# Attention and gated FFN in one kernel: order of the weight loads, of the first q and k transpositions and of the range check in the first sequence

## Chip, cores and metric

One Trainium2 chip, one core of it. The metric is the device time of one launch in microseconds (us), the median over several runs. Beside it there is one profiled execution, whose trace all durations below are taken from.

## What is computed

For each of four sequences of 512 tokens with 512 features, a layer norm feeds two branches, whose product is added to the input:

```python
xn = _layernorm(x, axis=-1)
s = _L0_attn_ref(xn, L0_attn_w_qkv, L0_attn_w_out, L0_attn_q_gamma, L0_attn_k_gamma)
g = _silu(_L0_ffn_ref(xn, L0_ffn_wq_gate, L0_ffn_s_gate, L0_ffn_wq_up, L0_ffn_s_up, L0_ffn_wq_down, L0_ffn_s_down))
x = x + s * g
```

The attention has 16 heads of 32 features: `qkv = xn @ w_qkv`; q and k are RMS-normalised per head and rotated by position; causal softmax; values; a product with `w_out`. The FFN is `down(silu(gate(xn)) * up(xn))` with 1408 hidden features; its three weight matrices come as int32 numbers with a zero point of 128 and one scale per row. All in float32.

## The kernel before

**Work and order.** One core does everything, and the order of the instructions on every engine is written out by hand (`manual_schedule`). A unit is a sequence b and a group g of four heads, 16 units in all. Each unit has two windows. In `hidden_window` PE computes a few of the 11 hidden blocks of the FFN: `hidden` (L583) with the gate weights, then with the up weights, each twice, with a coarse and a residual part of xn (`xh`, `xl`); ACT applies silu (L594), DVE multiplies (L600), ACT and POOL split the result into `h` (L601, L602). In the window that follows (`attention_window` for the first units) PE computes the scores of the unit (L450), DVE masks them and takes the row minimum (L471), ACT takes the exponential (L481), PE transposes the probabilities (L497) and multiplies them with v (L537); in between stand the FFN's down products (`contract`, L612) and the q, k, v product of the next unit (`product`, L368), whose result `rotate` normalises and rotates on ACT, DVE and POOL (L379 to L410). `Projection.turn` (L415 to L421) transposes q and k of the unit on PE, eight transpositions into two PSUM banks; ACT copies q out (L125), DVE copies k (L127). The scores need both.

**Preparing the weights.** In the first sequence the integer FFN weights are prepared beside the other work. `preparations` yields 34 blocks of up to 128x512 integers in the order in which the groups need them. `load_weights` (L241) has SP issue the load of a block into a free room (pieces of `arena`, `wout`, `oT`; the last two get their own contents later), `turn_weights` (L250) has ACT cast it to bf16 (L256) and SP issue a DMA that transposes it (L258), `finish_weights` (L261) has DVE subtract the zero point, write the result to `wgT`, `wuT` or `wdT` (L265), keep the block's largest value in a column of `largest`, and give the room back. `weights()` does a step of all three, twice in the first hidden window of the first sequence, three times in each of the next ones, and four times in each of its attention windows up to the last. A block's cast is asked for one or two steps after its load.

**Queues.** ACT, DVE, POOL and PE take their instructions in the written order; an instruction that waits holds up all behind it on its engine. SP issues almost all DMAs in the written order, too. The prologue (L933 to L966) loads x, the part of `w_qkv` for group 0, eight weight blocks, and at its end the rest of `w_qkv` for groups 1 to 3 (L961, four DMAs of 576 KB), `s_down` (L962) and three more blocks into `oT` (L963). It normalises x on DVE and POOL, transposes it on PE (`Norm.turn`, L340) and splits it (`Norm.cut`, L347: ACT writes `xh`, POOL the difference `xl`).

**First hidden window.** It has two blocks. The list `fills` (L697 to L704) says what stands between the products; in the first unit its third entry, between the gate and the up product of the second block, is `fresh.turn()` of q and k (L700). The ACT queue there reads: silu of block 0, cast of h, two casts of `oT` (L256), silu of block 1, q copy (L125), cast of h, casts of `oT` and of `wout` (L256), exponentials.

**Range check.** `find_wide` (L289) runs once, after the hidden window of group 2, when all weights are prepared: DVE takes the largest value over the columns (L293), PE transposes that one column (L295), DVE takes the largest of the 128 (L296) and writes the flag `wide` (L297). The flag decides at the end of the launch whether the whole work is done again in plain float32; with these inputs it is not. SP loads the flag into a register (L1438) right behind the load of `wout`.

Of the kernel before, what the change touches and what calls it, by code (L numbers as in the profile page):

```python
# [21 lines left out]
P = 128  # L22
# [4 lines left out]
NC = D // P  # L27
# [24 lines left out]
def interleaved(  # L52
# [27 lines left out]
    nc = tc.nc  # L80
# [23 lines left out]
    def bank_t(name):  # L104
        return ps_t.tile([P, 512], F32, tag="t", name=name)
# [50 lines left out]
    def load_wqkv(groups):  # L156
        for c in range(NC):
            nc.sync.dma_start(
                wqkv[:, c, :, groups, :],
                w_qkv[ts(c, P), :].rearrange("p (i g d) -> p i g d", i=3, g=NC)[:, :, groups, :],  # L160
            )
# [23 lines left out]
    def load_scales():  # L185
        srow = work("srow")
        at = 0
        for s in (s_gate, s_up):
            n = s.shape[0] // P
            nc.sync.dma_start(srow[at : at + n, 0:P], s.rearrange("(c p) -> c p", p=P))  # L190
            at += n
        return srow, at

    sdown = const.tile([P, D], F32, name="sdown")
# [46 lines left out]
    def load_weights(n):  # L241
        for _ in range(n):
            if todo and rooms:
                src, k, dst, name = todo.pop(0)
                room = rooms.pop(0)
                raw = room[:, : k * P]
                nc.sync.dma_start(raw.bitcast(U32), src.bitcast(U32))
                loaded.append((now[0], room, raw, k, dst, name))
# [29 lines left out]
    def weights(n=2):  # L278

        now[0] += 1  # L280
        for _ in range(n):
            if turning and now[0] - turning[0][0] >= 2:
                finish_weights()
        load_weights(n)
        for _ in range(n):
            if loaded and now[0] - loaded[0][0] >= 1:
                turn_weights()

    def find_wide():  # L289

        assert len(finished) == n_prep
        row = small.tile([P, 1], F32, tag="row", name="largest_row")
        nc.vector.tensor_reduce(row, largest, AX.X, ALU.max)  # L293
        tp = bank_t("largest_t")
        nc.tensor.transpose(tp[0:1, 0:P], row, ident)  # L295
        nc.vector.tensor_reduce(row[0:1, :], tp[0:1, 0:P], AX.X, ALU.max)  # L296
        nc.vector.tensor_single_scalar(wide, row[0:1, :], EXACT_MAX, ALU.is_ge)  # L297

    units = [(b, g) for b in range(B) for g in range(NC)]

# [122 lines left out]
    def swapped(b, g):  # L423


        return units[NC - 1] <= (b, g) < units[-1]
# [149 lines left out]
    def hidden(b, f, i, other=False):  # L576

        assert "gu"[i] + f"_{f}" in finished
        bank = (bank_t if other else bank_a)(f"h{i}_{b}_{f}")
        w = (wgT, wuT)[i]  # L580
        for a in (xh, xl):
            for c in range(NC):
                nc.tensor.matmul(  # L583
                    bank,
                    lhsT=w[:, c, ts(f, P)],
                    rhs=a[:, c, :],
                    start=(c == 0 and a is xh),
                    stop=(c == NC - 1 and a is xl),
                )
        return bank  # L590

    def gate(b, f, bank):
        sil = work(f"sil_{b}_{f}")
        nc.scalar.activation(sil, bank, AF.Silu, scale=scales[:, f : f + 1])  # L594
        return sil

    def gated(sil, f, bank, to):

        up = scales[:, NF + f : NF + f + 1]
        nc.vector.scalar_tensor_tensor(sil, bank, up, sil, ALU.mult, ALU.mult)  # L600
        nc.scalar.copy(to[:, 0, :], sil)  # L601
        nc.gpsimd.tensor_tensor(to[:, 1, :], sil, to[:, 0, :].bitcast(F32), ALU.subtract)  # L602
# [76 lines left out]
    def hidden_window(b, g, last, fresh, result, norm, beside):  # L679

        placed = last is not None and last.placed
        if result is not None and not placed:
            result.gate(0)

        def drain(i):
            if last is not None and not placed:
                last.turn(i, scalar=False)
                last.turn(i + 1, scalar=True)  # L690

        def turned(*tiles):
            if norm is not None:
                for t in tiles:
                    norm.turn(t)

        fills = [  # L697
            lambda: drain(0),
            lambda: drain(2),
            lambda: (last.spread_sums() if last is not None else None, fresh.turn()),  # L700
            lambda: turned(0, 1),
            lambda: turned(2),
            lambda: turned(3),
        ]  # L704
        for i, f in enumerate(chunks[g]):
            bank = hidden(b, f, 0, other=placed and i == 0)
            sil = gate(b, f, bank)
            if placed and i == 0:
                last.blocks(0, 1, 2)
            if fills:  # L710
                fills.pop(0)()
            if result is not None:
                for t in ((), (0, 1))[i] if placed else (2 * i + 1,):
                    result.gate(t)
            bank = hidden(b, f, 1, other=placed and norm is None and f == chunks[g][-1])
            gated(sil, f, bank, h[:, i])
            if placed and i == 0:
                last.blocks(3)
                last.spread()
            if fills:  # L720
                fills.pop(0)()
            if result is not None:
                for t in ((), (2, 3))[i] if placed else ((2,), ())[i]:
                    result.gate(t)
            for e in beside[i]:
                e()
            if b == 0:
                weights()
        if last is not None:
            last.turn_sums()  # L730
            if not placed:
                last.values()
# [200 lines left out]
    def prologue():  # L933
        norm, fresh = Norm(0), Projection(0, 0)
        load_weights(4)
        scales_in = load_scales()
        load_weights(4)
        for t in range(NT):
            norm.stats(t)
            norm.roots(slice(t, t + 1))  # L940
            if t:
                norm.apply(t - 1)
                norm.turn(t - 1)
        norm.apply(NT - 1)
        norm.turn(NT - 1)
        prepare_table()
        for t in range(NT):
            norm.cut(t)
        for _ in range(4):
            turn_weights()  # L950
        fresh.product(0)
        fresh.rotate(0)
        for _ in range(4):
            turn_weights()
        for t in range(1, NT):
            fresh.product(t)
            fresh.rotate(t)
            if t > 1:
                finish_weights()
                finish_weights()  # L960
        load_wqkv(slice(1, NC))  # L961
        nc.sync.dma_start(sdown, s_down.partition_broadcast(P))  # L962
        load_weights(3)  # L963
        now[0] += 1
        prepare_scales(*scales_in)
        return fresh  # L966

    fresh, last, norm, done = prologue(), None, None, None
    for u, (b, g) in enumerate(units):
        result = Result(b - 1) if g == 0 and b else None  # L970
        done = result or done
        beside = [[], [], []]
        if g == NC - 2 and b + 1 < B:
            for t in range(NT):
                load_x(b + 1, t)
            norm = Norm(b + 1)
            beside[1] += [lambda t=t: norm.stats(t) for t in (0, 1)]
            beside[2] += [lambda t=t: norm.stats(t) for t in (2, 3)]
            beside[2].append(lambda: norm.roots(slice(0, NT)))
        if g == NC - 1 and b + 1 < B:  # L980
            for i, tiles in enumerate(((0, 1), (2, 3))):
                beside[i] += [lambda t=t: norm.apply(t) for t in tiles]
        due = norm if g == NC - 1 and b + 1 < B else None
        hidden_window(b, g, last, fresh, result, due, beside)
        if g == 1 and b:
            for t in range(NT):
                done.store(t)
        if (b, g) == (0, NC - 1):
            nc.sync.dma_start(wout, w_out.rearrange("(c p) m -> p c m", p=P))
        if (b, g) == (0, NC - 2):  # L990
            find_wide()
        s = steps(b, g, fresh.v)
        if u + 1 == len(units):
            break
        fresh = Projection(*units[u + 1])
        if swapped(b, g):
            placed_window(b, g, last, s, fresh, due, result)
        else:
            attention_window(b, g, last, s, fresh, due)
        last = s[3]  # L1000
# [476 lines left out]
```

## Time and profile before

| | us |
|---|---|
| median of 3 runs | 678.67 (678.5 to 678.67) |
| the profiled execution, its own time | 679.54 |
| its span | 677.7 |

| first 180 us of the profiled execution | us |
|---|---|
| SP issues the loads of w_qkv for groups 1 to 3 (L158) | 27.75 to 30.39 |
| last q and k product of group 0 ends on PE | 26.25 |
| first hidden product starts | 26.34 |
| first scores of group 0 start | 42.09 |
| first hidden product of group 1 starts | 69.29 |
| first scores of group 1 start | 84.74 |
| first scores of group 2 start | 127.34 |
| first scores of group 3 start | 168.32 |

A profile line of a group reads: line, engine, operation, what it writes and reads, how many; in a timeline the start and the duration stand in front, and brackets at the end give the idle time of that engine just before and who ended it. A line of the waits reads: who waited for whom, us in total, how often, the longest. `PEclk` is the granted clock of TensorE, as a share of full speed. The page has further sections: a picture of 40 slices of 16.9 us, the DMA queues, and the chain of work that ended last.

### The profile page before, as it was taken

Reading aid. Unit: us, or ns where it says so; the run is one execution under the profiler, and the core shown is the slowest. Engines: PE = TensorE matmul, PEld = TensorE weight load, DVE = VectorE, ACT = ScalarE, POOL = GpSimd, SP = SyncE. Lnnn points to the kernel's source line nnn. Section 1 sums busy time; section 2 is a strip of 40 time slices with the busy share of each in tenths; the row PEclk is TensorE's granted clock in tenths of the full one; section 3 lists DMA queues with packets and bytes.
Section 4 is the critical chain, followed back from the end, with each engine's and each line's share of the span. In section 5 each row is a group of like instructions: output and inputs, shape, how many; then the busy total and the mean of one; then the engine's idle time right before and its main releaser. Section 6 shows DMA issues by size and latency. Waiting matters only on the chain.

```text
span 677.7 us, 11804 instructions
## 1 busy us (share of the span) xinstructions
PE 640.3 (94%) x4050; PEld 430.7 (64%) x4050; DVE 443.5 (65%) x1208; ACT 364.6 (54%) x931; POOL 319.9 (47%) x369
## 2 busy tenths in 40 slices
PE   4969999999999999999999999999999999999995
PEld 2645766668665576767665576766766466676752
DVE  3547677764886366777688357777588565757663
ACT  3456576554765064565757046464757246464660
POOL 4913536254472723537283641727284442726522
PEclk9969999999999999999999999999999999999998
DMA  7583644200222144322013323312223304222401
GB/s 250 149 209 94 180 97 107 94 1 1 48 55 68 50 124 100 74 47 46 22 43 79 94 44 106 102 46 48 64 47 78 94 1 125 47 63 48 125 1 68
DMA packets 48560, 53.19 MB, mean 78 GB/s; under 512 B 21334, under 2 KB 31852, under 8 KB 48492
## 3 DMA queue, kind: packets, MB, share of 16 engines
q1 hardware_dynamic: 47532, 51.93, 30.3%
q8 instruction: 34, 0.56, 0.3%
q10 hardware_dynamic: 960, 0.43, 0.2%
q14 instruction: 34, 0.28, 0.1%
HBM read 21.80 MB, written 4.19 MB: 38 GB/s over the span
## 4 chain that ended last, share of the span: by engine, by line
PE 84%; ACT 4%; DVE 4%; DMA 2%; POOL 2%; issue 2%; SPq 1%; DVEq 0%; ACTq 0%
PE qkv L368 25%; PE h L583 23%; PE dn L612 11%; PE so L655 8%; PE pv L537 6%; PE sc L450 5%; PE pt L497 4%; PE qkt L420 2%; POOL h L602 1%; DMA oT<-in_L_ffn_wq_up 1%; ACT arena L125 1%; DVE sil L600 1%; ACT arena L481 1%; PE xnt L344 1%; DMA x<-in_L_attn_x 1%
## 5 line engine op out<-in xcount | busy, mean ns | idle before, releaser
L481 ACT ACTIVATE arena<-arena,least 128x128 f32<-128x128 f32 (+3 forms) x256 | 141.2, 553 | 66.4 <-DVE least L471 66.3
L368 PE MATMUL qkv<-wqkv,xnT 128*128 128x384 f32 x512 | 173.6, 492 | 2.3 <-DVE least L471 2.3
L368 PEld LDWEIGHTS qkv<-wqkv,xnT 128*128 128x128 f32 x512 | 96.6, 193 | 68.6 <-issue 5.8
L471 DVE CUSTOM_DVE_ANT_0 arena<-sc,mask 128x128 f32<-128x128 f32 (+3 forms) x256 | 109.5, 486 | 31.0 <-PE sc L450 30.8
L408 POOL TENSOR_TENSOR qk<-qk,qs 128x256 f32<-128x256 f32 x64 | 46.7, 730 | 149.3 <-DVE qs L403 149.3
L602 POOL TENSOR_TENSOR h<-sil,h 128x512 fp32r<-128x512 f32 x44 | 57.8, 1314 | 116.2 <-ACT h L601 114.8
L315 POOL TENSOR_TENSOR ss<-ss,minus_half 128x8 f32<-128x8 f32 x64 | 106.7, 1668 | 5.3
L612 PE MATMUL dn<-wdT,h 128*128 128x512 f32 x352 | 100.0, 422 | 1.8 <-POOL h L602 1.8
L514 DVE STREAM_TRANSPOSE arena<-arena 128x384 f32<-128x384 f32 (+1 forms) x96 | 88.6, 977 | 12.3 <-PE pt L497 7.5
L612 PEld LDWEIGHTS dn<-wdT,h 128*128 128x128 f32 x352 | 63.5, 191 | 40.2 <-issue 20.4
L379 ACT ACTIVATE squares<-qkv 128x256 f32<-128x256 f32 x64 | 24.5, 382 | 119.7 <-PE qkv L368 99.0
L400 DVE TENSOR_TENSOR qk<-qkv,tab 128x256 f32<-128x256 f32 x64 | 27.0, 423 | 74.8 <-ACT v L380 74.4
L600 DVE SCALAR_TENSOR_TENSOR sil<-h,scales,sil 128x512 f32<-128x512 f32 x44 | 32.6, 740 | 56.8 <-PE h L583 45.0
L601 ACT CAST h<-sil 128x512 fp32r<-128x512 f32 x44 | 27.3, 620 | 69.8 <-DVE sil L600 69.8
L655 PE MATMUL so<-wout,oT 128*128 128x512 f32 x128 | 58.2, 593 | 0.0
L450 PE MATMUL sc<-kT,qT 32*128 32x512 f32 (+3 forms) x512 | 49.8, 474 | 5.8 <-ACT qT L125 5.8
L583 PE MATMUL h<-xh,wuT 128*128 128x512 f32 x176 | 50.1, 406 | 1.5 <-ACT qT L125 1.5
L497 PE MATMUL pt<-ident,arena 128*128 128x128 f32 x304 | 43.6, 279 | 7.2 <-ACT arena L125 7.1
L583 PE MATMUL h<-xh,wgT 128*128 128x512 f32 x176 | 49.1, 401 | 0.0
L497 PEld LDWEIGHTS pt<-ident,arena 128*128 128x128 f32 x304 | 35.0, 142 | 21.2 <-ACT arena L125 10.5
L583 PE MATMUL h<-xl,wuT 128*128 128x512 f32 x176 | 48.1, 395 | 0.0
L583 PE MATMUL h<-xl,wgT 128*128 128x512 f32 x176 | 48.1, 395 | 0.0
(90 smaller groups left out, 907.2 us busy)
## 6 DMA issues: line engine op xcount, KB each, us to landing
arena<-arena SPq DMA_DIRECT2D x48, 256.0 KB, 4.7
arena<-arena SPq DMA_DIRECT2D x48, 192.0 KB, 3.6
x<-in_L_attn_x SPq DMA_DIRECT2D x16, 256.0 KB, 4.7
out<-o SPq DMA_DIRECT2D x15, 256.0 KB, 4.5
xr<-in_L_attn_x SPq DMA_DIRECT2D x12, 256.0 KB, 4.1
wqkv<-in_L_attn_w_qkv SPq DMA_DIRECT2D x4, 576.0 KB, 4.8
wout<-in_L_ffn_wq_up SPq DMA_DIRECT2D x6, 256.0 KB, 3.1
wout<-in_L_ffn_wq_down SPq DMA_DIRECT2D x5, 256.0 KB, 3.9
```

What stands on the lines that cost most here:

```text
L315: nc.gpsimd.tensor_tensor(dst, dst, minus_half[:, : dst.shape[-1]], ALU.pow)
L368: nc.tensor.matmul(bank.rearrange("p (i d) -> p i d", i=3), lhsT=xnT[:, c, ts(t, P)], rhs=wqkv[:, c, :, self.g, :], start=(c == 0), stop=( ...
L408: nc.gpsimd.tensor_tensor(qk, qk, qs, ALU.add)
L450: nc.tensor.matmul(bank, lhsT=qT[rows, ts(self.t, P)], rhs=kT[rows, : self.keys], start=True, stop=True,)
L471: nc.vector.tensor_tensor_reduce(out=pr, in0=self.banks[j], in1=mask[:, N - self.keys :], scale=float(HD), scalar=3.0e38, op0=ALU.add, op1 ...
L481: nc.scalar.activation(pr, pr, AF.Exp, bias=least, scale=-1.0, accum_out=self.sums[:, self.t, j : j + 1],)
L497: nc.tensor.transpose(tp[:, ts(i * (self.t + 1) + k, P)], self.probs[n * self.per + i][:, ts(k, P)], ident,)
L514: nc.vector.transpose(piece(self.way, self.t + 1)[:, : HPG * self.keys].rearrange("p (c m k) -> p c m k", c=4, k=32)[:, :, j * n : (j + 1) * n
L583: nc.tensor.matmul(bank, lhsT=w[:, c, ts(f, P)], rhs=a[:, c, :], start=(c == 0 and a is xh), stop=(c == NC - 1 and a is xl),)
L602: nc.gpsimd.tensor_tensor(to[:, 1, :], sil, to[:, 0, :].bitcast(F32), ALU.subtract)
L612: nc.tensor.matmul(bank, lhsT=h[:, i, a, ts(t, P)], rhs=wdT[:, f, :], start=(i == 0 and a == 0), stop=(f == fs[-1] and a == 1),)
L655: nc.tensor.matmul(self.banks[t], lhsT=oT[:, g, ts(t, P)], rhs=wout[:, g, :], start=(g == 0), stop=(g == NC - 1),)
```

## The change

It touches four things, all in the first sequence. (1) The loads of w_qkv are parted by group: group 1 stands behind the three weight blocks at the end of the prologue instead of in front of them; group 2 and `s_down` follow after the first hidden window, group 3 after the second. (2) In the first unit q and k are turned at the end of the hidden window, after both blocks, instead of inside the second. On PE the eight transpositions thereby stand behind the eight products of the up half of block 1; on ACT the q copy stands behind the cast of h and the casts of `oT` and `wout`; on DVE the k copy stands behind the second L600 and two L265. (3) `find_wide` becomes a generator with two stops: its first reduction stays after the hidden window of group 2, the transposition and the rest come after the hidden window of group 3. (4) The prologue's `xl` is computed on DVE instead of POOL. Nothing is added to or taken from the arithmetic; SP issues 8 more DMAs (12 of 192 KB in place of 4 of 576 KB).

```diff
@@ find_wide
         nc.vector.tensor_reduce(row, largest, AX.X, ALU.max)
+        yield
         tp = bank_t("largest_t")
         nc.tensor.transpose(tp[0:1, 0:P], row, ident)
         nc.vector.tensor_reduce(row[0:1, :], tp[0:1, 0:P], AX.X, ALU.max)
         nc.vector.tensor_single_scalar(wide, row[0:1, :], EXACT_MAX, ALU.is_ge)
+        yield
@@ hidden_window
-            lambda: (last.spread_sums() if last is not None else None, fresh.turn()),
+            lambda: (last.spread_sums(), fresh.turn()) if last is not None else None,
...
-        if last is not None:
+        if last is None:
+            fresh.turn()
+        else:
             last.turn_sums()
@@ prologue
         for t in range(NT):
-            norm.cut(t)
+            norm.cut(t, nc.vector)
...
-        load_wqkv(slice(1, NC))
-        nc.sync.dma_start(sdown, s_down.partition_broadcast(P))
         load_weights(3)
+        load_wqkv(slice(1, 2))
@@ the loop over the units, after hidden_window
         if (b, g) == (0, NC - 1):
+            next(finding)
             nc.sync.dma_start(wout, w_out.rearrange("(c p) m -> p c m", p=P))
+        if b == 0 and 2 + g < NC:
+            load_wqkv(slice(2 + g, 3 + g))
+        if (b, g) == (0, 0):
+            nc.sync.dma_start(sdown, s_down.partition_broadcast(P))
         if (b, g) == (0, NC - 2):
-            find_wide()
+            finding = find_wide()
+            next(finding)
```

## The prediction

> **What bounds the kernel now.** I read the page first (busy shares, the 40 slices, the chain), then the waits of PE, then the timelines of the stretches where PE stood still, then a table of windows for the granted clock.
>
> ```profile
> PE 640.3 (94%) x4050; PEld 430.7 (64%) x4050; DVE 443.5 (65%) x1208; ACT 364.6 (54%) x931; POOL 319.9 (47%) x369
> PEclk9969999999999999999999999999999999999998
> ```
>
> PE carries the kernel; what it does not fill is 37 us. Slice 3 of PEclk (33.9 to 50.8 us) is the one dip before the end. The waits of PE between 20 and 180 us name what an edit in the first sequence can reach:
>
> ```profile
> PE sc L450 <- ACT qT L125: 5.8, 1, 5.8
> PE qkv L368 <- DVE least L471: 2.3, 4, 0.8
> PE largest_t L295 <- DVE largest_row L293: 1.2, 1, 1.2
> PE qkt L420 <- POOL qk L410: 1.1, 1, 1.1
> ```
>
> The timeline around the first (start, duration, engine, line) shows why ACT was late:
>
> ```profile
> 27.75 2.64 SPq L158 DMA_DIRECT2D wqkv<-in_L_attn_w_qkv  x4
> 30.43 0.66 SPq L962 DMA_DIRECT2D sdown<-in_L_ffn_s_down  x1
> 31.14 0.46 SPq L247 DMA_DIRECT2D oT<-in_L_ffn_wq_gate  x1
> 35.14 1.10 PE L583 MATMUL h<-xl,wuT 128*128 128x512 f32 x4
> 39.70 1.27 ACT L256 CAST oT<-oT 128x512 bf16<-128x512 uint32 x2 [6.86 <-DMA oT<-in_L_ffn_wq_gate]
> 41.46 0.57 ACT L125 COPY qT<-qkt 128x512 f32<-128x512 f32 x1
> 42.09 1.96 PE L450 MATMUL sc<-kT,qT 32*128 32x128 f32 x16 [5.85 <-ACT qT L125]
> ```
>
> ACT's next job is the cast of a weight block that queues behind 2.36 MB of wqkv and 0.26 MB of sdown; the q copy stands behind that cast on ACT, and PE's scores behind the q copy. PE idles from 36.24 to 42.09 us. That stall also costs clock:
>
> ```profile
> core 0: us, PE busy (x) PEld busy (x) DVE busy (x) ACT busy (x) POOL busy (x), PEclk, DMA share, GB/s
> 31.42:34.83 3.41, 2.33 (x15) 1.83 (x14) 2.38 (x6) 0.62 (x1) 3.29 (x3) 1.00 1.00 343
> 34.84:38.25 3.41, 1.40 (x6) 0.77 (x5) 0.26 (x1) 0.00 (x0) 0.00 (x0) 1.00 1.02 307
> 38.25:41.66 3.41, 0.00 (x0) 0.00 (x0) 0.07 (x1) 1.92 (x4) 0.00 (x0) 0.50 0.84 309
> 41.66:45.07 3.41, 2.98 (x19) 2.14 (x20) 3.17 (x15) 3.05 (x5) 1.27 (x1) 0.50 0.98 122
> 45.08:48.49 3.41, 3.41 (x12) 2.72 (x11) 1.72 (x7) 3.40 (x16) 0.00 (x0) 0.50 0.96 197
> 48.49:51.90 3.41, 3.41 (x13) 2.05 (x12) 1.32 (x3) 1.08 (x5) 0.00 (x0) 1.00 0.00 0
> ```
>
> The clock halves at 38.25 us, 2.0 us into the gap, and comes back at 48.49: three times 3.41 us apart, so it changes on a grid of 3.41 us. A stretch 68% busy kept the full clock, one 41% busy lost it; one 87% busy did not win it back, one wholly busy did. From 42.09 to 48.49 PE works at half speed: the 16 sc take 1.96 us (0.94 in the next group's window), eight dn 3.71 (8 x 0.234 = 1.87 at full clock).
>
> **The change, part by part.** Sums are against the profiled execution: 679.54 us, span 677.7. The runs' median, 678.67, lies 0.87 below it; the saving is carried over unchanged.
>
> *Queue.* The three oT loads are issued at 27.75 instead of 31.14. Data began to move at about 29.5 and ran at 321 to 336 GB/s in the next 4 us, so the 0.79 MB are in by about 32. ACT finishes its h cast (L601) at 32.22 + 0.62 = 32.84: its wait of 6.86 us goes. After them SP issues the first wqkv group (4 x 0.62 us, until about 31.7), then the wout block that frees at 32.81. 0.79 + 0.26 MB after 32 give a landing near 35.2.
>
> *Turning q and k later.* PE: the eight h matmuls of the second up block move ahead of the eight qkt. They start at 32.04 and take 2 x 0.93 us, to 33.9; POOL's last qk ends at 33.55, so the 1.07 us that PE waited there go too; qkt takes 0.87, to 34.8. ACT: after 32.84 two casts (1.27) to 34.11, sil 0.68 to 34.8, DVE's sil (L600) 0.75 to 35.6, h cast to 36.1, oT cast to 36.6, wout cast to 37.2 (pitch 0.52, as at 42.38 to 43.42), q copy 0.57 to 37.75. The change puts the q copy behind the casts of oT and of that wout block: the added wait is ACT's on the wout load (35.2, needed at 36.6; 1.4 us of cover; if the cover goes, q copy, scores and all of PE are late by the excess). DVE: wdT twice after 35.6, then the k copy, to about 37.5. Scores start at 37.8 instead of 42.09, and PE's gap is 34.8 to 37.8: 3.0 us.
>
> *The clock in that gap.* Here a rule and the row differ. The Trainium skill (TensorE: Matmul & The Clock Gate, Part 1, What's actually happening) has the clock drop after a wholly idle window of about 3.4 us, and says that the grid's place varies from run to run. By the rule a gap of 3.0 us costs no clock. The rows above show a drop after a stretch that was 41% busy. The runs lie within 0.17 us, though a grid in another place would move the half-speed time by up to 1.7 us; so I keep the grid. The gap then fills 34.84 to 38.25 but for 0.5 us: 15% busy, the clock falls at 38.25. The next stretch, to 41.66, is wholly busy if the scores start at 37.8, and the clock comes back there. By the rows: half of sc at full speed, the rest to 39.2; 5.2 dn at half speed to 41.66, 2.8 at full to 42.3; pt 0.45 (its exponentials are done by 40.7: table load 37.75 to 39.0, four of 0.39); qkv 2.6 to 45.35. Before, that product ended at 51.19: 5.85 us saved. By the rule it ends at 43.7 (pt waits for ACT until 41.1): 7.5 saved.
>
> *Does it last?* After 51.19 ACT had waited 2.33 us and DVE 1.93 for this product, so neither becomes the bound sooner. From there to 69.3 PE, DVE and ACT hand on to each other at full clock; no 3.41 us of that stretch are under 78% busy, so a shift against the grid costs no clock. All transfers hang on instructions that shift along.
>
> *The search parted.* At group 2 PE idles 1.24 us, as the transposition stands ahead of the scores and DVE does two st/mv pairs first:
>
> ```profile
> 124.81 1.08 PE L537 MATMUL pv<-arena,v 128*32 128x128 f32 x32
> 127.14 0.27 PE L295 MATMUL largest_t<-ident,largest_row 128*1 128x128 f32 x1 [1.24 <-DVE largest_row L293]
> 127.34 0.94 PE L450 MATMUL sc<-kT,qT 32*128 32x128 f32 x16
> ```
>
> Now the scores follow pv at 125.9. dn's last h part (POOL, done 127.31) is due at 126.7 + 5 x 0.234 = 127.9; ACT's table is in at 127.74, exponentials end by 129.3, pt needs them at 129.7. So 1.45 us are saved. The transposition (0.2) comes back at group 3, where its row is long done and DVE idles 1.91 us before the first mask. Net 1.25 us; between 0.9 and 1.45. From 127 to 175 the chain is nearly all PE, so it lasts. SP's load of the flag (L1438) now waits until about 169; behind it stand the arena copies, due only at 179.65.
>
> *At nothing.* xl on DVE: four of 0.68 (DVE's L351 later on) instead of 4.97 us of POOL, in DVE's idle 5.58 us before 19.20; POOL's qk sum started at 20.10 on DVE's sine products anyway. Were that cover gone, 2.7 us. The wqkv groups 2 and 3: 2.5 us of SP and 2.4 of DMA each at 330 GB/s, sdown 0.66. SP has nothing to issue from 47.2 to 53.6 and from 89.0 to 94.7, and the products that read them come 40 us later. Without cover the next weight loads would be 3 us late. 512-byte pieces instead of 1536: the first group, in such pieces, moved among other loads at 288 to 370 GB/s (4 to 8 us), so no price; half that rate would land the wout block near 38.3 and cost 1.7.
>
> **Sum.** 5.85 + 1.25 = 7.1: 672.4 for a profiled execution, 671.6 for the median.
>
> **Rivals.** (1) Clock back one stretch later, at 45.08, if sc does not count as fully busy or starts after 38.3: dn to 42.95, pt to 43.8, two qkv matmuls at half speed, six at 0.324: 47.0, 4.2 saved, + 1.25: 673.2. For it: the 87% stretch with sc in it did not win the clock back. Against: it began with 0.43 us of idle. (2) Clock never falls (grid elsewhere, or the gap shorter): 7.5 + 1.25: 670.0. Against it the 41% row. (3) Part of the wait returns, on ACT's weight casts or later in the group: 3 us kept, 675.7. (4) The change does nothing: the q copy waits as long for wout as it did for oT: within 0.2% of 678.7. (5) Slower: the same place, ACT's cast of the wout block ahead of the q copy. Scores start 1.2 us after that load lands. If it lands after 42.1, they start at 43.3 and the gain, search included, is gone; each us beyond is lost whole, and at 44.5 the time is 681. That needs 1.05 MB in 10 us, 100 GB/s where the trace shows over 320.
>
> **How the numbers follow.** Chances: forecast 0.47 (670.9 to 672.4 alone), (1) 0.23, (2) 0.13, (3) 0.08, (4) 0.03, (5) 0.06. A time within 0.2% (1.4 us) is what a measurement here can't tell from no change. The range takes in (2) and (1) with their bounds: 669.8 to 674.8. Faster 0.91, same 0.03, slower 0.06.
>
> **What would show it.** In the profile after: ACT's oT cast at about 32.8 without a wait; no wait of PE for POOL at qkt; sc near 37.8; PEclk at one half from 38.25 to 41.66 and nowhere else before the end; no wait of PE at largest_t; sc of group 2 straight behind pv. It is wrong if ACT's wout cast waits for its load, if the half clock lasts to 45, or if DVE or ACT, not PE, sets the pace from 40 to 46 us.

## The result and the profile after

| | before | after |
|---|---|---|
| median of 6 runs each, us | 678.67 (677.74 to 678.96) | 672.66 (669.79 to 673.74) |
| profiled execution, its own time / span, us | 679.54 / 677.7 | 673.09 / 671.3 |
| first hidden product of group 0 starts | 26.34 | 24.96 |
| first scores of group 0 | 42.09 | 37.16 |
| first hidden product of group 1 | 69.29 | 63.85 |
| first scores of group 2 | 127.34 | 120.45 |
| first scores of group 3 | 168.32 | 161.86 |

The ratio is 0.9908 (95% interval 0.989 to 0.9926): 6.0 us less. The single runs after lie 4 us apart, those of before 1.2; the shortest (669.79) has a mean granted clock of 0.997, the three longest (673.09 to 673.74) have 0.992. A stretch of 3.41 us at half speed takes 0.5 x 3.41 / 671 = 0.0025 off a run's mean clock, so by this estimate the ends differ by two such stretches.

From here on the changed file's lines stand two further down (L450 is now L452, L612 is L614). The page of the kernel after, busy shares and granted clock:

```profile
PE 639.0 (95%) x4050; PEld 429.9 (64%) x4050; DVE 446.2 (66%) x1212; ACT 364.6 (54%) x931; POOL 315.1 (47%) x365
PEclk9979999999999999999999999999999999999998
```

Slice 3 still dips, to 7 instead of 6: the clock still falls. The waits of PE between 20 and 180 us, after:

```profile
PE sc L452 <- ACT qT L125: 3.3, 1, 3.3
PE qkv L370 <- DVE least L473: 2.3, 4, 0.8
PE pt L499 <- ACT arena L125: 0.2, 1, 0.2
PE largest_t L296 <- ACT xnT L347: 0.2, 1, 0.2
```

The wait for POOL at `qkt` is gone, the one for DVE at `largest_t` has become 0.2 us for another engine. The scores still wait for the q copy, 3.3 us instead of 5.8. The timelines of SP, ACT and PE around it, after:

```profile
28.80 2.57 SPq L158 DMA_DIRECT2D wqkv<-in_L_attn_w_qkv  x4
31.46 0.55 SPq L247 DMA_DIRECT2D wout<-in_L_ffn_wq_up  x1
31.37 1.13 ACT L256 CAST oT<-oT 128x512 bf16<-128x512 uint32 x2
36.00 0.62 ACT L256 CAST wout<-wout 128x512 bf16<-128x512 uint32 x1 [0.96 <-DMA wout<-in_L_ffn_wq_up]
36.52 0.58 ACT L125 COPY qT<-qkt 128x512 f32<-128x512 f32 x1
37.16 1.66 PE L452 MATMUL sc<-kT,qT 32*128 32x128 f32 x16 [3.30 <-ACT qT L125]
38.75 3.78 PE L614 MATMUL dn<-wdT,h 128*128 128x512 f32 x8
```

The cast of `oT` has no bracket: its 6.86 us are gone. The cast of `wout`, which the q copy now stands behind, waits 0.96 us for a load that SP issued at 31.46, behind the four w_qkv loads of group 1: 4.5 us to landing. Eight dn take 3.78 us, as before: half speed. A table of windows of 3.41 us, cut 0.15 us ahead of the places where the clock changed (start and end, length, busy time of PE, PEld, DVE, ACT and POOL with their instructions, granted clock, DMA share, GB/s):

```profile
32.42:35.83 3.41, 1.35 (x10) 0.78 (x8) 2.56 (x6) 1.80 (x4) 3.08 (x3) 1.00 1.23 290
35.83:39.24 3.41, 2.08 (x17) 1.43 (x18) 0.40 (x3) 2.45 (x4) 0.04 (x1) 0.52 1.19 200
39.24:42.65 3.41, 3.41 (x10) 2.53 (x10) 2.59 (x15) 2.79 (x13) 0.00 (x0) 0.50 1.38 159
```

By the trace's record of the clock it falls at 35.98, in the gap, and comes back at 42.81, so it was low for two stretches, the second of them wholly busy. PE works at half speed from 37.16 to 42.81, 5.65 us (before: 42.09 to 48.49, 6.4). The edges do not lie where those of before lay.

The parted search, in PE's timeline of groups 2 and 3, after:

```profile
119.44 1.08 PE L539 MATMUL pv<-arena,v 128*32 128x128 f32 x32
120.45 0.94 PE L452 MATMUL sc<-kT,qT 32*128 32x128 f32 x16
...
161.66 0.27 PE L296 MATMUL largest_t<-ident,largest_row 128*1 128x128 f32 x1 [0.16 <-ACT xnT L347]
161.86 0.94 PE L452 MATMUL sc<-kT,qT 32*128 32x128 f32 x16
```

Group 2's scores follow pv directly; the transposition stands in group 3.

**Where the 6.4 us of the profiled execution went.** The first hidden product starts 1.38 us earlier; from there to the first hidden product of group 1 it takes 38.89 us instead of 42.95 (4.06); scores of group 1 to those of group 2 41.10 instead of 42.60 (1.50 saved), group 2 to 3 41.41 instead of 40.98 (0.43 given back). 1.38 + 4.06 + 1.50 - 0.43 = 6.51; 0.05 went back between the first hidden product and the first scores of group 1, and the remaining 0.06 later. The 1.38 is mostly no effect of the change. The first q, k, v product starts 0.50 us earlier (13.25 instead of 13.76) and takes 0.88 less (11.60 instead of 12.48); the clock came to full speed at 15.50 in this execution and at 17.78 in the one before. In kernels without the move of `xl` the first hidden product started between 24.61 and 26.34, in those with it between 24.81 and 25.87.

### The profile page after: what moved, and what is told of

It reads as the page before. It is cut to its first block, busy times and chain, and to the rows that moved or that the text cites. A ratio compares the mean times of both kernels' runs of the same rounds, so it can differ in the third digit from the quotient of the medians.

```text
span 671.3 us, 11815 instructions
## 1 busy us (share of the span) xinstructions
PE 639.0 (95%) x4050; PEld 429.9 (64%) x4050; DVE 446.2 (66%) x1212; ACT 364.6 (54%) x931; POOL 315.1 (47%) x365
## 4 chain that ended last, share of the span: by engine, by line
PE 85%; ACT 5%; DVE 5%; issue 2%; DMA 2%; POOL 2%; SPq 0%; DVEq 0%; ACTq 0%
PE qkv L370 25%; PE h L585 24%; PE dn L614 11%; PE so L657 8%; PE pv L539 6%; PE sc L452 5%; PE pt L499 4%; PE qkt L422 2%; POOL h L604 1%; ACT arena L125 1%; DVE sil L602 1%; ACT arena L483 1%; PE xnt L346 1%; DMA x<-in_L_attn_x 1%; DMA wout<-in_L_ffn_wq_up 1%
## 5 line engine op out<-in xcount | busy, mean ns | idle before, releaser
L614 PE MATMUL dn<-wdT,h 128*128 128x512 f32 x352 | 100.0, 422 | 1.8 <-POOL h L604 1.8
L614 PEld LDWEIGHTS dn<-wdT,h 128*128 128x128 f32 x352 | 63.5, 191 | 40.2 <-issue 21.0
L452 PE MATMUL sc<-kT,qT 32*128 32x512 f32 (+3 forms) x512 | 49.5, 474 | 3.3 <-ACT qT L125 3.3
```

The lines of the kernel that those rows point to most:

```text
L452: nc.tensor.matmul(bank, lhsT=qT[rows, ts(self.t, P)], rhs=kT[rows, : self.keys], start=True, stop=True,)
L614: nc.tensor.matmul(bank, lhsT=h[:, i, a, ts(t, P)], rhs=wdT[:, f, :], start=(i == 0 and a == 0), stop=(f == fs[-1] and a == 1),)
```

## The experiments

The theory going in: the load order gives the gain, the search about 1 us, and the later turning by itself costs, since the q copy then stands behind the casts of two blocks, one of them late. What the gap costs beyond its length is the clock behind it. The rival: the later turning helps, and part of the gain is its own.

Useful for reading all runs: from the first hidden product of group 0 to that of group 1 (H), the first scores, and whether the clock fell.

| kernel | median us (runs) | ratio, 95% | first hidden / first scores | H | clock low |
|---|---|---|---|---|---|
| before (its first profile) | | | 26.34 / 42.09 | 42.95 | 38.3 to 48.5 |
| e1 load order alone | 672.15 (5) | 0.9917, 0.9904 to 0.9931 | 25.99 / 35.73 | 36.39 | never |
| e2 search alone | 676.88 (20) | 0.9986, 0.9978 to 0.9994 | 24.66 / 41.26 | 42.91 | 39.0 to 45.8 |
| e3 later turning alone | 680.4 (5) | 1.004, 1.0027 to 1.0054 | 24.64 / 43.84 | 45.36 | 38.1 to 48.4 |
| e4 after, turned ahead of the casts | 669.97 (4) | 0.9886, 0.9871 to 0.9901 | 24.81 / 34.92 | 35.96 | never |
| f1 after again | 672.77 (5) | 0.9923, 0.991 to 0.9937 | 25.36 / 37.44 | 39.18 | 37.1 to 43.9 |
| f2 after, gap filled | 670.18 (4) | 0.9883, 0.9868 to 0.9898 | 25.14 / 37.01 | 35.97 | never |
| f3 after, old place of turning | 671.44 (4) | 0.9903, 0.9888 to 0.9918 | 25.87 / 35.59 | 36.80 | never |
| f4 after, wout load ahead of w_qkv | 671.23 (4) | 0.9896, 0.9881 to 0.9911 | 24.96 / 36.10 | 36.81 | 36.3 to 39.7 |
| g1 both mends | 668.88 (4) | 0.9861, 0.9846 to 0.9876 | 25.06 / 35.16 | 35.12 | never |
| g2 before, gap filled | 678.97 (13) | 1.0008, 0.9999 to 1.0016 | 24.61 / 42.83 | 44.68 | 45.2 to 48.7 |
| g3 before, oT loads ahead, rest whole | 678.44 (13) | 1.0003, 0.9995 to 1.0012 | 25.60 / 35.54 | 41.83 | 44.2 to 47.7 |
| g4 xl on DVE alone | 678.14 (13) | 0.9991, 0.9983 to 1.0 | 25.37 / 41.87 | 43.19 | 40.4 to 47.2 |

The runs of one letter were made on one chip beside runs of the kernel before (medians 677.77, 677.87 and 678.47). "Clock low" is read from the one trace of each kernel, ahead of the fall at the very end. The mean clocks of the single runs agree: all runs of e1, e4, f2, f3 and g1 have 0.997 or more, those of the kernel before 0.989 to 0.994.

**e1 and e2, one part alone.** e1 takes the new load order into the kernel before:

```diff
-        load_wqkv(slice(1, NC))
-        nc.sync.dma_start(sdown, s_down.partition_broadcast(P))
         load_weights(3)
+        load_wqkv(slice(1, 2))
...
+        if b == 0 and 2 + g < NC:
+            load_wqkv(slice(2 + g, 3 + g))
+        if (b, g) == (0, 0):
+            nc.sync.dma_start(sdown, s_down.partition_broadcast(P))
```

> Only the order of the loads is changed; q and k are turned inside the second block as before. Theory (the saving is the load order's, and the later turning costs part of it): ACT's wait for the oT load goes, the q copy is done before PE ends the up products, PE's gap ahead of the first scores shrinks from 5.85 us to under 1 us, the clock stays full, and the first product of the next group ends about 6.7 us earlier: 672.0 us, all but the search of the whole gain or more. Rival (the later turning is needed too): PE still waits for POOL at qkt and for a bank or the q copy at the scores, 3 to 4 us saved, about 675.

e2 takes the two stops of `find_wide`:

```diff
+        yield
         tp = bank_t("largest_t")
...
+            next(finding)
```

> Only the search for large weights is parted. Theory: the 1.45 us between pv and the scores of group 2 go, and about 0.45 us come back at group 3: 1.0 us saved, 677.7 us. Rival (another engine sets the pace there): the scores start earlier but PE waits later in the window for DVE or ACT, nothing saved: 678.7 us.

Measured: 672.15 and 676.88. The load order alone gives 5.6 us, nearly all that the whole change gave; the search 0.9. Together that would be 6.5, and the whole change gives 6.0 in the first measurement and 5.1 in f1. The waits of PE in e1 between 20 and 60 us:

```profile
PE qkv L368 <- DVE least L471: 1.4, 2, 0.8
PE qkt L420 <- POOL qk L410: 1.0, 1, 1.0
PE sc L450 <- DVE sil L600: 0.5, 1, 0.5
PE dn L612 <- DVE wdT L265: 0.3, 1, 0.3
```

Of the 5.8 us in front of the scores 0.5 are left, with work on either side; the wait for POOL is the old one (1.1 before). The clock stays full.

**e3, the later turning alone.**

```diff
-            lambda: (last.spread_sums() if last is not None else None, fresh.turn()),
+            lambda: (last.spread_sums(), fresh.turn()) if last is not None else None,
...
-        if last is not None:
+        if last is None:
+            fresh.turn()
+        else:
             last.turn_sums()
```

> Only the turning of q and k is moved behind both hidden blocks; the loads stay in the old order. Theory: the q copy now stands behind two more casts, one of them of a wout block that is the last in the queue; the scores start 2.5 us or more later than before (about 44.6 instead of 42.1 us): about 681 us. Rival (turning later saves the 1.07 us that PE waits for POOL and the q copy was never what PE waited for): 677.6 us.

Measured: 680.4, slower than before. PE's wait for the q copy is now

```profile
PE sc L450 <- ACT qT L125: 10.3, 1, 10.3
```

In the old load order ACT's silu of block 1 stands behind the cast of the late `oT` block (here at 38.96). Now the cast of h and two more casts stand ahead of the q copy as well: it starts at 43.22 instead of 41.46, and the scores at 43.84 instead of 42.09. PE's wait grows by more than that, since its up products are done before it.

**e4, the turning between its old and its new place:** behind both blocks' products, ahead of the last casts.

```diff
                 e()
+            if last is None and i == len(chunks[g]) - 1:
+                fresh.turn()
             if b == 0:
                 weights()
-        if last is None:
-            fresh.turn()
-        else:
+        if last is not None:
             last.turn_sums()
```

> The changed kernel with one difference: q and k are turned behind the second block's products but ahead of the casts of the last two weight blocks, so ACT's q copy does not stand behind the cast that waits for the wout load. Theory: the scores start about 2 us earlier than in the changed kernel (35.1 instead of 37.2 us), the gap of PE is 1.7 us and half a grid stretch stays busy, so the clock stays full; PE then waits some 1.5 us for the exponentials; about 3.4 us less than the changed kernel: 669.2 us. Rival (the clock falls all the same, or the wait for wout only moves to the exponentials and costs as much): 672 us.

Measured: 669.97, 2.8 us below f1 (on another chip; against the kernel before on the same chip e4 saves 7.8 us and f1 5.1). Here PE waits 1.36 us in front of the scores, and for a different engine:

```profile
34.92 0.94 PE L452 MATMUL sc<-kT,qT 32*128 32x128 f32 x16 [1.36 <-DVE wdT L265]
```

The 16 sc take 0.94 us: full clock. So the late place on PE is good (H 35.96 against 36.80 in f3, at the old place); the place behind ACT's casts is bad.

**f1, the changed kernel again, and f2, its gap filled** with 12 products of 128x512 behind the turning:

```diff
         if last is None:
             fresh.turn()
+            idle = ps_d.tile([P, D], F32, tag="dn", name="idle")
+            for k in range(12):
+                nc.tensor.matmul(idle, lhsT=wgT[:, 0, 0:P], rhs=xh[:, 0, :], start=True, stop=True)
```

> The changed kernel unaltered, to see its spread. Theory (the time left over from the turn's gap is set by where the clock's grid falls on it): about 672.6 us, single runs 669.8 to 673.8, and a run is shorter the higher its mean granted clock. Rival (the spread comes from the loads, not from the clock): the same median, but runs of one mean clock as far apart as all of them.

> The changed kernel, with twelve 128x512 products (2.8 us at full clock) put on PE behind the turning of q and k, into a bank that nobody reads: their result is not used, and they fill most of the 3.3 us gap. Theory (the gap costs clock behind it: scores to the q, k, v product at half speed for up to 5.5 us, worth up to 2.7 us): clock full until the end, about 670.2 us, all runs within 1 us. Rival (the clock is a symptom, ACT or DVE sets the pace from the scores on): 672.6 or above.

Measured: 672.77 with single runs of 672.17 to 673.73, and 670.18 with runs of 669.81 to 670.45. The scores start equally late in both, 12.08 and 11.87 us behind the first hidden product: in f2 PE still has no useful work in the gap. Yet from those scores to the scores of the next token tile f1 takes 10.22 us and f2 7.21. The windows of f1:

```profile
33.60:37.01 3.41, 0.36 (x4) 0.12 (x2) 2.48 (x6) 1.87 (x4) 1.62 (x2) 1.00 1.13 235
37.01:40.42 3.41, 2.98 (x19) 2.10 (x20) 1.28 (x10) 2.62 (x7) 0.00 (x0) 0.51 1.80 210
40.42:43.83 3.41, 3.41 (x11) 2.73 (x10) 1.85 (x8) 2.75 (x12) 0.00 (x0) 0.50 0.73 177
```

and of f2:

```profile
33.60:37.01 3.41, 2.95 (x15) 2.06 (x13) 2.27 (x6) 2.28 (x5) 1.71 (x2) 1.00 1.42 235
37.01:40.42 3.41, 3.41 (x29) 2.68 (x30) 2.46 (x14) 3.37 (x12) 0.00 (x0) 1.00 1.07 203
```

The same 3.41 us, 11% busy in one and 87% in the other. That the clock, not DVE or ACT, sets the pace behind the gap is thereby shown: 3.0 us of the profiled execution, 2.6 of the median. f1's own spread (1.6 us) did not settle the expectation that a shorter run always has a higher mean clock: four of its runs, 672.59 to 673.73, all have 0.992; the fifth and shortest, 672.17, has 0.995.

**f3, the whole change but the old place of turning** (the reverse of e3's diff):

> The changed kernel with q and k turned at the old place, inside the second block; load order, parted search and xl on DVE as changed. Theory (the later turn by itself costs, since the q copy now stands behind two casts that wait for data): queue 672.15 less the search's 0.9, 671.2 us, runs within 1 us, clock full. Rival (the later turn takes away the wait of PE for POOL and so helps): above 672.7.

Measured: 671.44, runs of 671.19 to 671.72, all below f1's shortest (672.17). So in this company the later turning costs 1.3 us at the median. But it does so through the clock: with the clock full (f2) H is 35.97, less than f3's 36.80.

**f4, the wout load ahead of the w_qkv loads of group 1:**

```diff
         load_weights(3)
-        load_wqkv(slice(1, 2))
...
         load_weights(n)
+        if behind is not None:
+            behind()
...
-                weights()
+                weights(behind=(lambda: load_wqkv(slice(1, 2))) if g == 0 and i == 0 else None)
```

> The changed kernel with the w_qkv loads of group 1 issued behind the first wout block's load instead of in front of it; all else as changed. Theory (ACT's wait of 0.96 us for the wout block, which the q copy stands behind, comes from those four loads in front): no wait at that cast, scores about 1 us earlier, gap 2.3 us, 671.3 us (670 to 672.3, by the clock). Rival (the wout block is late by its own transfer): wait stays near 1 us, 672.6 us.

Measured: 671.23. ACT's wait is gone, the q copy starts at 35.47 and the gap is 2.52 us. The clock falls in it all the same, but the scores (36.10) start before the next stretch begins, and it is back at 39.70:

```profile
32.88:36.29 3.41, 0.89 (x11) 0.65 (x13) 2.56 (x6) 2.57 (x6) 2.38 (x2) 1.00 0.91 295
36.29:39.70 3.41, 3.41 (x21) 2.37 (x20) 1.31 (x11) 2.80 (x10) 0.00 (x0) 0.50 1.12 124
```

One stretch at half speed here, two in f1 and in the first profile after. Scores to scores of the next tile: 8.78 us, between f2's 7.21 and f1's 10.22.

**g1, both mends together** (the diffs of e4 and f4):

> The changed kernel with both mends: q and k turned behind the products of both blocks but ahead of the last casts of weights (as in the run e4), and the w_qkv loads of group 1 behind the first wout block's load (as in f4). Theory: ACT's wait of 0.74 us at the wout cast in e4 goes, so the exponentials and the first transposed probabilities come 0.7 us earlier: 669.3 us, runs within 0.6 us, clock full. Rival (that wait lay beside DVE's masks or PE's products): 669.97 as e4.

Measured: 668.88, runs of 668.38 to 669.63; ratio 0.9861 (0.9846 to 0.9876), the best version, ahead of both kernels. The casts no longer wait; what is left is PE's 1.50 us for DVE's `wdT` in front of the scores:

```profile
35.16 0.94 PE L454 MATMUL sc<-kT,qT 32*128 32x128 f32 x16 [1.50 <-DVE wdT L265]
```

**g2, the kernel before with its gap filled** by 22 such products behind the hidden products of the first unit (the same lines as in f2).

> The kernel before, with 22 products of 128x512 (5.15 us at full clock) put on PE behind the hidden products of the first unit, into a bank that nobody reads: their result is not used, and they fill most of the 5.85 us gap. It keeps the wait and takes away the clock's fall. Theory (from the first scores to those of the next token tile before took 10.3 us, and 7.2 with the clock full in f2): 3.1 us less than before, 674.8 us. Rival (behind the gap DVE and ACT set the pace): within 0.5 us of before.

Measured: 678.97, no gain: the theory's 3.1 us did not come, and the rival's number did. In the profiled execution the first hidden product came 1.73 us earlier than in the profile before and the load of `oT` no earlier, so the gap was 7.6 us and the filling covered 5.3. The clock fell at 45.24, behind the first scores. Windows cut at its own edges:

```profile
38.42:41.83 3.41, 2.15 (x10) 1.39 (x8) 0.00 (x0) 1.32 (x3) 0.00 (x0) 1.00 0.61 223
41.83:45.24 3.41, 2.03 (x20) 1.39 (x20) 2.91 (x14) 3.05 (x6) 1.28 (x1) 1.00 0.48 100
45.24:48.66 3.42, 3.42 (x11) 2.75 (x11) 2.13 (x10) 3.41 (x14) 0.00 (x0) 0.50 0.83 208
```

From the first scores to the end of the next q, k, v product it took 8.37 us instead of 9.10, but the scores came 0.74 us later (42.83), behind a later `oT`. Nor could f2's 3.1 us carry over. In the old order ACT has the cast of h, two casts of blocks and a table load to do between the q copy and the first exponential, which starts 3.26 us behind the first scores in the kernel before and in g2, and 1.28 in f2 (in this order):

```profile
45.35 0.40 ACT L481 ACTIVATE arena<-arena,least 128x128 f32<-128x128 f32 x1
46.09 0.40 ACT L481 ACTIVATE arena<-arena,least 128x128 f32<-128x128 f32 x1
38.29 0.40 ACT L483 ACTIVATE arena<-arena,least 128x128 f32<-128x128 f32 x1
```

PE's transpositions need four of them. An estimate from the rows of before: the fourth ends at 46.91, the last transposition (0.2) and the product (2.6) follow, 49.7 instead of 51.19; a full clock would have been worth some 1.5 us there. Three of g2's thirteen runs have a mean clock of 0.998 or 0.999, as high as where it never fell, and took 677.81, 678.14 and 679.06: none near 674.8. Why they gained nothing at all is not shown, as only one execution has a trace.

The second of g2's windows, 60% busy, lost the full clock; in g1 one that was 56% busy kept it:

```profile
33.03:36.45 3.42, 1.92 (x24) 1.30 (x23) 2.89 (x9) 2.59 (x6) 2.26 (x2) 1.00 0.92 291
```

So the busy share of PE alone does not say when it falls.

**g3, the three oT loads ahead, w_qkv and s_down whole behind them:**

```diff
-        load_wqkv(slice(1, NC))
-        nc.sync.dma_start(sdown, s_down.partition_broadcast(P))
         load_weights(3)
+        load_wqkv(slice(1, NC))
+        nc.sync.dma_start(sdown, s_down.partition_broadcast(P))
```

> The kernel before with only the three oT loads moved in front of the w_qkv loads of groups 1 to 3 and s_down, which stay whole (2.36 MB and 0.26 MB) and stay there. Theory (the loads in front of the first wout block decide: 2.03 MB more than in e1, some 6 us at 340 GB/s): the q copy is early, but the exponentials stand behind ACT's cast of the wout block, which lands near 43 us; PE's transposition of the probabilities waits about 5 us and the clock falls: 676 to 678 us. Rival (the three oT loads are all that matters): 672.2 as e1.

Measured: 678.44, the same as before. ACT's next cast takes the wait over, and the exponentials stand behind it:

```profile
41.63 0.62 ACT L256 CAST wout<-wout 128x512 bf16<-128x512 uint32 x1 [3.98 <-DMA wout<-in_L_ffn_wq_up]
```

So moving three loads to the front gives nothing; the gain needs what stands behind them parted and put off, w_qkv of groups 2 and 3 and s_down: 1.57 + 0.26 = 1.83 MB (the expectation's 2.03 was miscounted).

**g4, `xl` on DVE alone** (`norm.cut(t)` becomes `norm.cut(t, nc.vector)` in the prologue):

> The kernel before with only xl moved from POOL to DVE in the prologue. Theory (DVE has room there and the next step waits for other work): same as before, 677.9 us within 0.5. Rival (q and k are ready earlier or DVE is late): over 1 us off, to either side.

Measured: 678.14, 0.3 us below the kernel before; the interval of the ratio reaches from a gain of 1.2 us to none. So the move is worth little or nothing, as forecast.

## Why the prediction was right, and where it was not

The direction, the place and the range were right: 672.66 in 669.8 to 674.8, 1.1 us above 671.6. Of the forecast's 7.1 us its own steps gave 5.1 in the profiled execution (4.06 + 1.07), and f1 measures 5.1 as well; the 6.0 of the first medians has an interval of 5.0 to 7.5. By its steps:

- **Queue.** Right: no wait at the `oT` cast. e1 shows it alone, 5.6 us.
- **No wait for POOL at `qkt`.** Right, but what it frees on PE is lost in front of the scores.
- **"1.4 us of cover" for the wout load.** Wrong: a wait of 0.96 us. In the profiled execution ACT came for the block at 35.04 and not 36.6 (the prologue was quicker by 1.4), and the block landed at 36.0 and not 35.2. 1.4 - 1.56 - 0.8 = -0.96. It was foreseen as a thing to watch ("it is wrong if ACT's wout cast waits for its load"). Half the DMA rate, feared for the 512-byte pieces, did not come: 290 GB/s in that stretch, 307 in the nearest one before.
- **Scores at 37.8.** 11.46 us behind the first hidden product in the forecast, 12.20 measured; PE's gap is 3.3 us instead of 3.0.
- **"So I keep the grid."** This is the step that failed. The edges lie elsewhere in every profile: the clock fell at 38.26 before, 35.98 after, 37.11 in f1, 36.30 in f4, which leaves 0.7, 1.8, 3.0 and 2.2 modulo 3.41. The Trainium skill (TensorE: Matmul & The Clock Gate, Part 1, What's actually happening) says that the window is free-running and its place varies between runs; on that it was right and the forecast, which rejected it, was not. The forecast's reason was that the runs of before lie within 0.17 us. Those were three runs. All six of the first comparison lie within 1.2 us, the 33 beside g within 2.6, and their mean clock is not one either: six have 0.989 (678.67 to 679.80), the others 0.992 to 0.994 (677.23 to 678.97). So the time at half speed varied in the kernel before, too. The execution that the forecast summed against (679.54, 0.989) was of the slower kind, and carrying its whole saving over to the median left that out.
- **What makes the clock fall.** The forecast took the row (41% busy, lost) over the same section's wholly idle window, and this held: after, a stretch 35% busy between the clock's own edges lost it (40% as cut in the table), in f4 one of 26%. Counted over all fourteen traces with windows laid on each trace's edges, the 2638 that kept the full clock were all at least 50% busy, and of the 23 that lost it 22 were at most 41% busy; the other is g2's, 60%. On the way back 90% busy was not enough (f1), and wholly busy was, in all nine cases.
- **"Back at 41.66", 3.41 us at half speed.** Its size failed: 6.8 us low, of which 5.65 with work, because the scores came after the edge at 35.98 and so the first stretch was partly idle. That is what rival (1) described, and the product ended 20.79 us behind the first hidden product, not 19.01: 4.06 us saved instead of 5.85, near its 4.2. 0.74 of the 1.79 between them is the later scores; the other 1.05, by subtraction, is the clock. f4 shows the forecast's own case. (The eight dn of before took 3.78 us by the trace, not 3.71, which changes nothing.)
- **Does it last.** Right: 4.06 us at the product, 4.06 at group 1.
- **Search.** 1.50 saved, 0.43 given back (0.2 forecast; the transposition also waits 0.16 for ACT's copy of `xnT`): net 1.07 instead of 1.25, 0.9 alone.
- **At nothing.** g4 for `xl`. The loads of groups 2 and 3 delay no product: PE's waits at qkv are 2.3 us in all, as before.
- **Slower.** The mechanism exists (g3, e3), but the load landed at 36.0, far from the 42.1 at which it would have decided.

The likeliest number came out well partly by luck: it credits the later turning with a part of the gain, while at its new place, behind ACT's casts, it costs 1.3 us. The forecast never priced the change without it. What stays open: the exact condition under which the clock falls (56% kept in g1, 60% lost in g2), and the clock's share in the kernel before, for which there is only the estimate of 1.5 us.

## What to carry to other kernels

When a load in a queue is late, look at every job that its consumer engine has behind it, and move the critical copy ahead of all of them; moving only the first late load passes the wait on to the next one (g3). Value a gap on PE by its length and by the half-speed work behind it (here a gap of 3.3 us cost up to another 3.0; less where another engine is late behind it, as ACT in g2), and take the clock's place against the gap as chance: a choice that keeps the gaps short and separate, as e4 and g1 do, is worth more than its sum of idle time says. Three runs that lie close together are no proof that a random thing is fixed; look at more runs, and at their mean clocks.

## What the hardware showed unexpectedly

- The place of the clock's grid changes from execution to execution, and the time follows it where a stall of about a stretch's length meets it: the six first runs of the changed kernel spread over 4 us, the four of f2, whose gap is filled, over 0.6.
- At the start PE runs at half speed too, though the view shows 1.00: the trace's record of the clock has its first entry, the step to full speed, at 17.78 in the profile before, and nothing ahead of it. There the weight loads of the first q, k, v product stand 0.64 us apart up to 17.60, then 8.03 / 25 = 0.32 us. That step lies between 14.22 (e3) and 17.78 (before) in the fourteen traces, and the 32 matmuls of the product take 11.12 us in e3, 11.60 after, 12.48 before and 12.65 in f3. Together with the product's start (12.92 to 13.76) this spreads the first hidden product over 24.61 to 26.34.
- The wout load of 256 KB, issued behind four of 192 KB, took 4.5 us to landing after; ahead of them in f4 it was issued at 31.43 and in by 34.95, when its cast began without a wait.
